# Moving the attention's weights by DMA into a one-pass tile before TensorE turns them

## The chip, the cores and the metric

The kernel runs on one core of a Trainium2 chip. The metric is device time in microseconds (us) of one execution. A core has a matrix engine (TensorE, PE in the profile, with its weight loads listed as PEld), a vector engine (VectorE, DVE), a scalar engine (ScalarE, ACT), a general engine (GpSimd, POOL) and a synchronisation engine (SyncE, SP). Each of them works off its own list of instructions in order and waits on semaphores that the others raise. DMA transfers are issued by an instruction on one of these engines (here SP, whose issues appear as SPq, and POOL) and then run by themselves on 16 DMA engines that all transfers share.

## The reference

One decoder layer in float32 on four sequences of 512 rows of width 512, with three sublayers, each behind a layer norm (without learned scale) and each added to the residual stream x:

```
q, k, v = x@Wq+bq, x@Wk+bk, x@Wv+bv       # 16 heads of width 128
y = softmax(q k^T / sqrt(128)) v          # here q, k are laid out so that the
x = x + y @ Wo + bo                       # softmax runs over feature pairs of a head
x = x + gamma * cross_attention(layernorm(x), ctx, ctx)      # 8 heads
x = x + (silu(h @ w1q') * (h @ w3q')) @ w2q',  h = layernorm(x)   # ternary weights
```

In the first sublayer the transposes put the 128 features of a head on both axes of the scores: for each sequence and head there is a 128 x 128 score matrix, summed over the 512 rows of the sequence. Its softmax is applied to the values, and the result goes through Wo. The change is in this sublayer alone, between its softmax and the product with Wo and the values.

## The kernel before, in words

**The attention.** The work is done per sequence b (0 to 3) and per group j (0 to 3) of four heads, so in 16 rounds. Since both axes of the scores are features, the kernel first forms the Gram matrix G of the normalised rows (`gram_upper`, matmuls `pg`, and `gram_rest`, which mirrors its lower blocks with TensorE transposes `gt`). A round then computes `u`, rows times Wo's part (`values_out`, PSUM names `pu`); `y`, G times Wk's part (`keys_of`, `py`); `m`, Wv's part times u (`values_of`, `pm`); and the scores (`scores`, line 503). `scores` takes Wq's part times y into one PSUM bank `sc` (L509, 16 matmuls of 128 x 128), finds the row maxima on DVE (L517), writes the exponentials to the tile `e` on ACT (L524, four, one for each head), and divides them by their row sums on DVE (L535, four, in place). `e` is 128 x 512: four heads side by side.

`turned` (L540) belongs to the next round: TensorE transposes the four 128 x 128 blocks of `e` into a PSUM bank `pe` (L126 in `transpose_blocks`, a matmul with `e`'s block as the loaded weights and the constant `ident` as the moving side), and ACT copies the bank to `eT`. `output` (L545) then multiplies `eT` with `m` (`po`) and adds to the accumulators `acc`. For j = 0, 1, 2 the four transposes stand between the `pu` and the `py` products of the following round; for j = 3 they stand inside the next sequence's Gram products, after `pg_1`, and for the last sequence after the loop.

**Number formats.** The larger products are made in TensorE's one-pass format (fp32r): every operand is split into a high part h, a low part l and a part d, so that a product of three such terms is as good as a float32 one (lines L336, L337, L348; `tri_of` makes the parts, ACT copies the first sum out of PSUM at L343 into a tile `t`, DVE totals the two at L358). The transposes, the scores, `po`, and some products of sequence 0 (L370) are in plain float32.

**Sequence 0** is special: it also prepares the weights. SP loads raw pieces of 256 KB (`load`, L196; `v_last`, `k_raw` and so on), DVE folds a correction into them (L255), ACT and DVE make the parts, and POOL issues the DMAs that keep them in DRAM for the later sequences (`keep`, L274) and small ones for the biases (L251). The output bias row is loaded once for each sequence into a tile `bo_bc` (`bias_rows`, L841; by SP for b = 0, by POOL for b > 0), and in sequence 0 it is added to the four accumulators by DVE in round j = 1 (`biased`, L857), between that round's totals of `u`.

**Buffers.** Tiles of one tag share slots in turn: a tile that takes a slot waits until the tile that was there before it has been read for the last time. The pool `a_y` (tag `y`, five slots of 128 x 512) holds a round's four `y`, the four blocks of G for b > 0, and `bo_bc`. The pool `a_t` has three slots (`t` copies and `u` totals), `e` has one slot of its own, and the eight PSUM banks go round in the same way.

**Order.** The order on each engine isn't that of the source. A planner places instructions by the modelled times of what they need (a few stretches are held in place by hand, with `issue_after` and `manual_schedule`). So a tile that asks for another slot can move instructions that the source doesn't touch, on every engine and in the DMA queues.

**The rest.** While sequences 1 to 3 go through the attention, the cross-attention of the sequence before (`xs`, `xp`, `xo`; its loads are POOL issues at L689) and the quantisation of the feed-forward weights are mixed in. At the end come the feed-forward products (L1084, L1119).

Of the kernel before, what the change touches and what calls it, by code (L numbers as in the profile page):

```python
# [11 lines left out]
F32 = mybir.dt.float32  # L12

F32R = mybir.dt.float32r
# [5 lines left out]
P = 128  # L20
B, T, D = 4, 512, 512
# [4 lines left out]
GW = HG * DH  # L26
# [13 lines left out]
def decoder_layer_kernel(  # L40
# [16 lines left out]
    nc = tc.nc  # L57

    const = ctx.enter_context(tc.tile_pool(name="const", bufs=1))
# [6 lines left out]
    def bank(name):  # L66
        return psum.tile([P, 512], F32, tag="bank", name=name)
# [8 lines left out]
        for n in ("w1", "w3", "w2")  # L76
    }
    scales = {n: const.tile([P, 3], F32, name=f"scales_{n}") for n in ("w1", "w3", "w2")}
    ident = const.tile([P, P], F32, name="ident")
    ones = const.tile([P, P], F32, name="ones")  # L80
    eps = const.tile([P, 1], F32, name="eps")
    gam = const.tile([P, 1], F32, name="gam")
# [39 lines left out]
    def transpose_blocks(dst, src, name, on_act):  # L122

        pt = bank(name)
        for k in range(4):
            nc.tensor.transpose(pt[:, ts(k, P)], src[:, ts(k, P)], ident)  # L126
        pv = pt.rearrange("p (k t) -> p k t", k=4)
        if on_act:
            nc.scalar.copy(dst, pv)  # L129
        else:  # L130
            nc.vector.tensor_copy(dst, pv)
# [18 lines left out]
    def apool(name, bufs):  # L150
        return apools.enter_context(tc.tile_pool(name=name, bufs=bufs))

    x3p, xnp, g3p, u3p = apool("a_x3", 12), apool("a_xn", 4), apool("a_g3", 1), apool("a_u3", 12)
    yp, tp = apool("a_y", 5), apool("a_t", 3)
# [60 lines left out]
    def exact(n, b, j):  # L215
        return b > 0 or j >= FIRST[n]
# [85 lines left out]
    def weights(n, b, j, wp):  # L302
        def wtile(name, dt=F32R):
            return wp.tile([P, GW], dt, tag="w", name=name)

        if n == "q":
            return [load(wtile(f"q_{b}_{j}_{k}", F32), kept_q[j][ts(k, P), :]) for k in range(KC)]
        tris = []
        make = b == 1 and not exact(n, 0, j)
        one = one_of(recent[0]) if make else None  # L310

        def part(p, k):
            t = wtile(f"{n}{p}_{b}_{j}_{k}")
            if p != "d" or not make:
                load(t.bitcast(F32), kept[n, j, p][ts(k, P), :])
            return t

        halves = [(part("h", k), part("l", k)) for k in range(KC)]
        for k in range(KC):
            tri = Tri(*halves[k], part("d", k))  # L320
            if make:
                nc.vector.scalar_tensor_tensor(
                    tri.d, tri.l.bitcast(F32), one, tri.h.bitcast(F32), ALU.mult, ALU.subtract
                )
                nc.gpsimd.dma_start(kept[n, j, "d"][ts(k, P), :], tri.d.bitcast(F32))
            tris.append(tri)
        return tris
# [57 lines left out]
    def normed(b, xs, by_chunk):  # L385

        mv = small.tile([P, NG, 2], F32, tag="mv", name=f"mv_a_{b}")

        def finish(part, std):
            rstd = inverse(std, f"a_{b}_{part[0]}")  # L390
            for g in part:
                normalize(xs[g], xs[g], mv[:, g, 0:1], rstd[:, g - part[0] : g - part[0] + 1])
                last = nc.vector.memset(xs[g][:, D - 1 : D], 1.0).ins
            return last

        parts = [(g,) for g in range(NG)] if by_chunk else [tuple(range(NG))]
        due = []
        for part in parts:
            for g in part:
                if b > 0:  # L400
                    settle(xs[g])
                moments(mv[:, g, :], xs[g], f"a_{b}_{g}")
            if b == 0:
                with tc.issue_after(mark["std"]):
                    nc.scalar.copy(accs[part[0]], xs[part[0]])
            due.append((part, std_of(mv[:, part[0] : part[-1] + 1, :], f"a_{b}_{part[0]}")))
            if len(due) > 1:
                finish(*due.pop(0))
        return finish(*due.pop())
# [93 lines left out]
    def scores(b, j, w, ys):  # L503

        scale = (S if exact("k", b, j) else 1.0) / math.sqrt(DH)
        sc = bank(f"sc_{b}_{j}")
        for g in range(NG):
            for k in range(KC):
                nc.tensor.matmul(  # L509
                    sc[:, ts(g, DH)],  # L510
                    lhsT=w[k][:, ts(g, DH)],
                    rhs=ys[k][:, ts(g, DH)],
                    start=(k == 0),
                    stop=(k == KC - 1),
                )
        nmax = small.tile([P, NG], F32, tag="nmax", name=f"nmax_{b}_{j}")
        mark["nmax"] = nc.vector.reduce_max(  # L517
            nmax, sc.rearrange("p (h k) -> p h k", h=NG), axis=AX.X
        ).ins
        nc.vector.tensor_scalar(nmax, nmax, -scale, None, ALU.mult)  # L520
        e = ep.tile([P, GW], F32, name="e")
        den = small.tile([P, NG], F32, tag="den", name=f"den_{b}_{j}")
        for g in range(NG):
            nc.scalar.activation(  # L524
                e[:, ts(g, DH)],
                sc[:, ts(g, DH)],
                AF.Exp,
                bias=nmax[:, g : g + 1],
                scale=scale,
                accum_out=den[:, g : g + 1],  # L530
            )
        rden = small.tile([P, NG], F32, tag="rden", name=f"rden_{b}_{j}")
        nc.vector.reciprocal(rden, den)
        for g in range(NG):
            nc.vector.tensor_scalar(  # L535
                e[:, ts(g, DH)], e[:, ts(g, DH)], rden[:, g : g + 1], None, ALU.mult
            )
        return e

    def turned(b, j, e):  # L540
        eT = ep.tile([P, NG, DH], F32, tag="eT", name=f"eT_{b}_{j}")
        transpose_blocks(eT, e, f"pe_{b}_{j}", True)
        return eT
# [136 lines left out]
    def cross(b, cx, cin, cpp, cpt):  # L680
# [71 lines left out]
        def transpose_rows(n, h, ps):  # L752
            if h == 0:
                pts[n] = cpt.tile([P, NC, T], F32, tag="pt", name=f"pt_{b}_{n}")
            for i in range(2):
                transpose_blocks(
                    pts[n][:, :, ts(2 * h + i, P)], ps[i], f"xp_{b}_{n}_{h}_{i}", i or h
                )

        def turn_values(c):  # L760
            vals[c] = cin.tile([P, NC, P], F32, tag="vals", bufs=1, name=f"vals_{b}_{c}")
            transpose_blocks(vals[c], rows[c], f"vt_{b}_{c}", True)
# [70 lines left out]
    accs = [accp.tile([P, D], F32, tag="acc", name=f"acc_0_{g}") for g in range(NG)]  # L833
    with tc.manual_schedule(engines={nc.vector.engine}):
        rows_done = normed(0, xs, True)
    make_identity(nc, ident)
    cpools = ctx.enter_context(ExitStack())

    def bias_rows(b):
# [25 lines left out]
    for j in range(HG):  # L865
# [58 lines left out]
        if j == HG - 1:  # L924
            normed(1, xs, False)
        e = scores(0, j, w, ys)
        keep_weights("q", j, w, first, gates["q"])
        if j == 0:
# [48 lines left out]
    for b in range(1, B):  # L977
# [18 lines left out]
        for j in range(HG):  # L996
            u3 = values_out(b, j, x3, weights("o", b, j, wp), tick)
            if j > 0:
                waiting[2] = turned(*waiting[:3])
            ys = keys_of(b, j, g3, weights("k", b, j, wp), tick)  # L1000
            if j > 0:
                output(*waiting)
            else:
                accs = accumulators(b, bo_bc)
            if j == HG - 2:
                xs = rows_of(b + 1)
            if j == HG - 1 and b + 1 < B:
                normed(b + 1, xs, False)
                x3 = parts_of(b + 1, xs)
            elif j == HG - 1:  # L1010
                for t in xs:
                    settle(t)
                ffn_0 = prepare_ffn(0, xs)
                for _ in range(NC):
                    next(ffn_0)
            ms = values_of(b, j, weights("v", b, j, wp), u3, tick)
            e = scores(b, j, weights("q", b, j, wp), ys)
            if j == 0:
                biased(accs, bo_bc)
            waiting = [b, j, e, ms, accs]  # L1020
# [48 lines left out]
    for b in range(B):  # L1069
# [39 lines left out]
        for c in range(NC):  # L1109
            if b == B - 1:  # L1110
                y = last_ys[c]
            else:
                y = fwk.tile([P, D], F32, tag="y", bufs=1, name=f"yo_{b}_{c}")
# [63 lines left out]
```

## Time and profile before

Three runs took 1152.76, 1149.95 and 1154.46 us; the median is 1152.76 us. The profiled execution spans 1150.0 us from its first to its last instruction.

| What | Value |
|---|---|
| Median of three runs | 1152.76 us |
| Runs, lowest to highest | 1149.95 to 1154.46 us |
| Span of the profiled execution | 1150.0 us, at a granted TensorE clock of 0.999 |
| PE busy | 1140.7 us, 99% of the span, 5310 matmuls |
| DVE busy | 818.7 us, 71% |
| ACT busy | 523.5 us, 46% |
| POOL busy | 295.9 us, 26% |
| Moved by DMA | 270.68 MB, mean 235 GB/s |

How to read the profile: a row of the timeline gives the start in us, the busy time in us, the engine, the line of the kernel, the operation, the output tile `<-` the inputs, and how many instructions are put together; a bracket at the end tells how long the engine stood idle before and what ended the wait. A row of a tile's view gives durations in ns as minimum/median/maximum, then the first and the last start. Matmuls overlap in the engine's pipeline: a matmul's own duration is longer than the step from one start to the next, and the step is what a row of many costs. A row of DMA issues gives the number of transfers, KB for each, and the median us from issue to landing. The chain is followed backwards from the last instruction, at each step to what released it.

### The profile page before, as it was taken

What the parts mean: (1) busy time and instruction counts of PE and PEld (TensorE: products, weight loads), DVE (VectorE), ACT (ScalarE), POOL (GpSimd) and SP (SyncE); (2) the same over time, 40 slices, a digit from 0 to 9 for tenths busy, and PEclk for the clock granted to TensorE, in tenths of its full rate; (3) what the DMA queues carried; (4) which work ended last, traced back from release to release, by engine and by line L of the source; (5) the groups of instructions that cost most, each with busy time, mean ns of one, the idle gap of its engine ahead of it and who ended that gap; (6) DMA issues with size and microseconds to landing.
All of it is one profiled execution on the core that took longest, in us unless ns stands there. A gap on an engine that the chain in (4) does not pass through costs nothing.

```text
span 1150.0 us, 16662 instructions
## 1 busy us (share of the span) xinstructions
PE 1140.7 (99%) x5310; PEld 858.6 (75%) x5310; DVE 818.7 (71%) x1818; ACT 523.5 (46%) x1071; POOL 295.9 (26%) x534
## 2 busy tenths in 40 slices
PE   9999999999999999999999999999999999999998
PEld 5486585787778767877776787777778877777886
DVE  6857766978788965969696769788857856536242
ACT  4534334354535442644354445445355768534020
POOL 3435433433133232213221422122113212000000
PEclk9999999999999999999999999999999999999999
DMA  9999996998889769988986798799791422122100
GB/s 332 306 344 337 345 314 225 324 319 280 281 281 308 261 201 325 312 272 276 321 291 215 256 334 271 254 330 325 268 304 40 122 79 65 48 73 72 64 1 37
DMA packets 146177, 270.68 MB, mean 235 GB/s; under 512 B 18276, under 2 KB 49300, under 8 KB 146090
## 3 DMA queue, kind: packets, MB, share of 16 engines
q1 hardware_dynamic: 112218, 164.93, 43.4%
q0 software_dynamic: 33872, 104.70, 26.8%
q8 instruction: 42, 0.69, 0.2%
q14 instruction: 45, 0.37, 0.1%
HBM read 206.62 MB, written 62.93 MB: 234 GB/s over the span
## 4 chain that ended last, share of the span: by engine, by line
PE 96%; DMA 2%; DVE 1%; issue 1%; ACT 0%; POOL 0%; SPq 0%; DVEq 0%; POOLq 0%; ACTq 0%
PE h L1084 13%; PE y L1119 7%; PE xo L770 5%; PE xp L126 5%; PE po L548 5%; PE pm L370 5%; PE sc L509 5%; PE pg L430 3%; PE xs L727 3%; PE xs L726 2%; PE pu_2h L336 1%; PE pu_1d L348 1%; PE py_3h L336 1%; PE py_3h L337 1%; PE pu_2h L337 1%; PE py_2h L337 1%
## 5 line engine op out<-in xcount | busy, mean ns | idle before, releaser
L1084 PE MATMUL h<-fxh,t 128*128 128x512 f32 (+1 forms) x352 | 139.6, 397 | 0.0
L1084 PE MATMUL h<-fxl,t 128*128 128x512 f32 (+1 forms) x352 | 137.4, 390 | 0.0
L737 ACT ACTIVATE p<-xs,xnmax 128x512 f32<-128x512 f32 x128 | 87.2, 689 | 84.8 <-PE xp L126 68.2
L731 DVE TENSOR_REDUCE xnmax<-xs 128x1 f32<-128x512 f32 x128 | 83.5, 684 | 19.3 <-PE xs L727 19.3
L1084 PEld LDWEIGHTS h<-fxh,t 128*128 128x128 f32 (+1 forms) x352 | 65.0, 185 | 15.4 <-issue 1.1
L1084 PEld LDWEIGHTS h<-fxl,t 128*128 128x128 f32 (+1 forms) x352 | 65.0, 185 | 14.7 <-issue 0.2
L1119 PE MATMUL y<-t,gh 128*128 128x512 f32 (+1 forms) x176 | 69.3, 394 | 0.0
L1119 PE MATMUL y<-t,gl 128*128 128x512 f32 (+1 forms) x176 | 68.8, 391 | 0.0
L129 ACT COPY pt<-xp 128x512 f32<-128x512 f32 x96 | 54.1, 595 | 31.0 <-PE xp L126 31.0
L126 PE MATMUL xp<-ident,p 128*128 128x128 f32 x512 | 66.5, 273 | 0.0
L126 PEld LDWEIGHTS xp<-ident,p 128*128 128x128 f32 x512 | 59.3, 140 | 9.4 <-issue 2.4
L770 PE MATMUL xo<-pt,vals 128*64 128x512 f32 x256 | 61.5, 599 | 0.0
L1097 DVE SCALAR_TENSOR_TENSOR gf<-h,scales_w,sl 128x512 f32<-128x512 f32 (+1 forms) x44 | 32.9, 747 | 39.8 <-PE h L1084 36.4
L749 DVE TENSOR_SCALAR p<-p,xrden 128x512 f32<-128x512 f32 x128 | 56.7, 486 | 2.9
L548 PE MATMUL po<-m,eT 128*128 128x512 f32 x128 | 57.6, 593 | 0.0
L1093 ACT ACTIVATE sl<-h,scales_w 128x512 f32<-128x512 f32 (+1 forms) x44 | 30.1, 688 | 58.7 <-PE h L1084 58.5
L689 POOL DMA_DIRECT2D xd<-x_a x64 | 33.8, 532 | 88.6 <-DVE qs L710 64.5
L370 PE MATMUL pm<-u,v_raw 128*128 128x512 f32 x128 | 55.6, 592 | 0.0
L727 PE MATMUL xs<-kl,qs 128*128 128x512 f32 x128 | 50.1, 391 | 0.5 <-DVE kl L714 0.5
L138 POOL CAST gh<-gf 128x512 fp32r<-128x512 f32 (+1 forms) x24 | 15.8, 660 | 134.9 <-DVE gf L1097 119.7
L726 PE MATMUL xs<-kh,qs 128*128 128x512 f32 x128 | 50.1, 392 | 0.0
L139 DVE TENSOR_TENSOR gl<-gf,gh 128x512 fp32r<-128x512 f32 (+1 forms) x44 | 30.4, 690 | 26.3 <-POOL gh L138 19.3
(313 smaller groups left out, 2897.6 us busy)
## 6 DMA issues: line engine op xcount, KB each, us to landing
oh<-kept_oh SPq DMA_DIRECT2D x48, 256.0 KB, 5.9
ol<-kept_ol SPq DMA_DIRECT2D x48, 256.0 KB, 6.2
kh<-kept_kh SPq DMA_DIRECT2D x48, 256.0 KB, 5.2
kl<-kept_kl SPq DMA_DIRECT2D x48, 256.0 KB, 5.9
vh<-kept_vh SPq DMA_DIRECT2D x48, 256.0 KB, 6.6
vl<-kept_vl SPq DMA_DIRECT2D x48, 256.0 KB, 6.9
q<-kept_q SPq DMA_DIRECT2D x48, 256.0 KB, 6.6
od<-kept_od SPq DMA_DIRECT2D x44, 256.0 KB, 6.8
```

Source lines behind the costliest of these rows:

```text
L126: nc.tensor.transpose(pt[:, ts(k, P)], src[:, ts(k, P)], ident)
L370: nc.tensor.matmul(p, lhsT=lhs(k)[:, ts(i, P)], rhs=rhs(k), start=(k == 0), stop=(k == 3))
L509: nc.tensor.matmul(sc[:, ts(g, DH)], lhsT=w[k][:, ts(g, DH)], rhs=ys[k][:, ts(g, DH)], start=(k == 0), stop=(k == KC - 1),)
L548: nc.tensor.matmul(po, lhsT=eT[:, g, :], rhs=ms[g], start=True, stop=True)
L726: nc.tensor.matmul(sc, lhsT=q[:, ts(m, P)], rhs=kh, start=True, stop=False)
L727: nc.tensor.matmul(sc, lhsT=q[:, ts(m, P)], rhs=kl, start=False, stop=True)
L731: nc.vector.reduce_max(nmax[:, i : i + 1], scs[i], axis=AX.X)
L737: nc.scalar.activation(p, scs[i], AF.Exp, bias=nmax[:, i : i + 1], scale=xscale, accum_out=den[:, i : i + 1],)
L749: nc.vector.tensor_scalar(ps[i], ps[i], rden[:, i : i + 1], None, ALU.mult)
L770: nc.tensor.matmul(po[half, :], lhsT=vals[c][:, l, half], rhs=pt[j][:, l, :], start=(l == 0), stop=(l == NC - 1),)
L1084: nc.tensor.matmul(ph[:r, :], lhsT=t[:, block(i, k)], rhs=fxT[j][:, k, :], start=(k == 0 and j == 0), stop=(k == KC - 1 and j == 1),)
L1119: nc.tensor.matmul(py, lhsT=g[i][j][:r, ts(c, P)], rhs=t2[:r, i, :], start=(i == 0 and j == 0), stop=(i == NHC - 1 and j == 1),)
```

## The change

The divided exponentials are copied by a DMA, issued on POOL, from `e` to a new tile `moved` (named `e_b_j`) of type fp32r in the `y` pool, and the transposes read `moved` in the one-pass format instead of `e` in float32. For that the identity matrix is needed as an fp32r tile: it is built in a float32 tile `eye` (also in the `y` pool) and copied by POOL to `ident_r`; `ident` becomes a float32 view of the same bytes, for all other transposes.

```diff
-    ident = const.tile([P, P], F32, name="ident")
+    ident_r = const.tile([P, P], F32R, name="ident")
+    ident = ident_r.bitcast(F32)
...
         pt = bank(name)
         for k in range(4):
-            nc.tensor.transpose(pt[:, ts(k, P)], src[:, ts(k, P)], ident)
+            if src.dtype == F32R:
+                nc.tensor.transpose(pt[:, ts(k, P)].bitcast(F32R), src[:, ts(k, P)], ident_r)
+            else:
+                nc.tensor.transpose(pt[:, ts(k, P)], src[:, ts(k, P)], ident)
...
                 e[:, ts(g, DH)], e[:, ts(g, DH)], rden[:, g : g + 1], None, ALU.mult
             )
-        return e
+        moved = yp.tile([P, GW], F32R, tag="y", name=f"e_{b}_{j}")
+        nc.gpsimd.dma_start(moved.bitcast(F32), e)
+        return moved
...
-    make_identity(nc, ident)
+    eye = yp.tile([P, D], F32, tag="y", name="eye")[:, :P]
+    make_identity(nc, eye)
+    nc.gpsimd.tensor_copy(ident_r, eye)
```

There are 16 such DMAs, each of 128 rows of 2 KB (256 KB), and 64 transposes that change their format. Only `e` is an fp32r source: the transposes of G, of the cross-attention and of the feed-forward inputs stay as they are. The change adds no slot to the `y` pool.

Line numbers in this document are those of the kernel before.

## The prediction

> **What bounds the kernel now.** I read the busy times first, then the clock slices and the chain, then the groups of the tiles `pe` and `y`, and last the timeline around the 16 turns.
>
> ```profile
> span 1150.0 us, 16662 instructions
> PE 1140.7 (99%) x5310; PEld 858.6 (75%) x5310; DVE 818.7 (71%) x1818; ACT 523.5 (46%) x1071; POOL 295.9 (26%) x534
> PEclk9999999999999999999999999999999999999999
> PE 96%; DMA 2%; DVE 1%; issue 1%; ACT 0%; POOL 0%; SPq 0%; DVEq 0%; POOLq 0%; ACTq 0%
> ```
>
> PE works through the whole span at full clock, and the chain is PE for 96%. The holes between its matmuls add up to some 4 us. So only two things move the time: PE work that becomes shorter, and any wait put ahead of a matmul. Everything else counts only where it makes PE wait.
>
> ```profile
> L126 PEld LDWEIGHTS pe<-ident,e x64: 138/140/143, 77.2 to 847.7; 128*128 128x128 f32 x64
> L126 PE MATMUL pe<-ident,e x64: 270/272/329, 77.4 to 847.7; 128*128 128x128 f32 x64
> 839.37 1.04 PE L126 MATMUL xp<-ident,p 128*128 128x128 f32 x8
> 81.54 1.98 PE L348 MATMUL py_1d<-k_d,gd 128*128 128x512 f32 x8
> ```
>
> The reader is to see the price of a turn (rows 2 and 3: eight take 1.04 us and the last is 272 ns long, so a step is (1.04−0.27)/7 = 110 ns) and of the one-pass format (row 4: (1.98−0.39)/7 = 227 ns for 512 columns).
>
> **What becomes shorter.** 64 turns change format. If 128 columns cost a quarter of 227 ns, a step is 57 ns: 64 × 52 = 3.3 us gained. No row has a one-pass product of 128 columns, so the ends lie far apart. One end is 3.3 us. In the middle is nothing: the step stays at 110 ns, limited by the weight load. The other end is a loss: a float32 product of that shape takes two halves of 112 ns in the scores, and at 224 ns the turns would cost 64 × 0.114 = 7.3 us more. I take the 3.3, by the nearest row of that format, and because the turn's weight load is shorter (140 ns) than the other loads of 128 columns (187 to 192).
>
> The Trainium skill, "TensorE: Matmul & The Clock Gate", section "LDWEIGHTS (loading the stationary operand)", speaks against that: a load costs its number of columns divided by 1.2, 107 ns for 128 columns, whatever the product behind it. By it the gain would be nothing and the sum below 3.3 us higher.
>
> **What is added.** Before, the turn reads `e` itself. Now a POOL DMA of 256 KB stands between, and `moved` takes the fifth slot of the `y` pool.
>
> *Waits for the DMA.* From the end of the division (L535) to the first turn there are 7.1 to 13.9 us in 14 of the 16 rounds. POOL's transfers of this size land in 2.3 to 3.8 us in quiet stretches, 4 to 7 in sequences 1 to 3, 6 to 8 in sequence 0. So 14 are hidden; closest are the first round of sequence 0 and of sequence 1 (about 1 us over), bounded at 0 to 1 us each, taken as 0. Two have no slack:
>
> ```profile
> 194.78 0.87 DVE L535 TENSOR_SCALAR e<-e,rden 128x128 f32<-128x128 f32 x4
> 196.10 0.60 PE L126 MATMUL pe<-ident,e 128*128 128x128 f32 x4
> 843.17 0.88 DVE L535 TENSOR_SCALAR e<-e,rden 128x128 f32<-128x128 f32 x4
> 843.60 0.63 PE L126 MATMUL pe<-ident,e 128*128 128x128 f32 x3
> 847.74 0.33 PE L126 MATMUL pe<-ident,e 128*128 128x128 f32 x1
> keys<-in_kv_dram POOLq DMA_DIRECT2D x1, 256.0 KB, 3.1
> bo_bc<-in_bo_dram POOLq DMA_DIRECT2D x1, 256.0 KB, 3.8
> xc<-x_a POOLq DMA_DIRECT2D x1, 256.0 KB, 7.1
> ```
>
> The last three are issues: two of 190 to 206 us, one of 838 to 856.
>
> - Sequence 0, j = 3: `e` is done at 195.65. An issue of 0.35 and a landing of 3.1 give 199.1, against 196.10: a stall of 3.0 us (2.2 with the quickest landing of 2.3, 3.8 with `bo_bc`'s 3.8). Behind the turns on PE stand the last two rows of the Gram matrix.
> - Sequence 3, j = 3: three turns before stood at 843.6, within the cross-attention, ahead of the last block's division. In the changed order all four stand together after `xo_3`, which PE reaches at about 847.4, so most of the latency is covered. `e` is done at 844.05; the issue comes behind `xc` on POOL's queue, and `xc` landed after 7.1 us at 848.2. A transfer behind it lands between 848.3 and 851.5: a stall of 0.9 to 4.1, I take 2.5. Nothing follows the turns on PE that could go ahead of them.
>
> *The bias row in sequence 0.* This is the largest part, and it isn't in the edited lines. With `e_0_0` in the fifth slot, `bo_bc_0` has to take that of `y_0_0_0`, and in the changed program its SP load goes from 45.00 us to behind the loads of `k_raw_2`, ahead of `v_last_2`. DVE's four additions of it (L857) move behind `u_1_1` and ahead of `u_1_2`.
>
> ```profile
> 45.00 0.65 SPq L841 DMA_DIRECT2D bo_bc<-in_bo_dram  x1
> 76.45 0.56 SPq L196 DMA_DIRECT2D v_last<-in_wv_dram  x1
> 61.88 0.68 DVE L857 TENSOR_TENSOR acc<-acc,bo_bc 128x512 f32<-128x512 f32 x1
> 62.55 1.89 DVE L857 TENSOR_TENSOR acc<-acc,bo_bc 128x512 f32<-128x512 f32 x3
> 72.03 1.29 DVE L358 SCALAR_TENSOR_TENSOR u<-pu_1t,pu_1d 128x512 f32<-128x512 f32 x2 [2.73 <-PE pu_1d L348]
> 77.43 0.60 PE L126 MATMUL pe<-ident,e 128*128 128x128 f32 x4
> 78.33 0.40 PE L336 MATMUL py_1h<-k_h,gh 128*128 128x512 f32 x1
> ```
>
> The load is issued at about 76.4 and lands at 81.1 (4.7 us, as `k_raw` and `v_last` beside it). The additions take 2.57 us and `u_1_2` 0.65: it is done at 84.4 instead of 72.7. Queued behind them on DVE are `u_1_3`, the gate and the four `v_raw` corrections. ACT waits as well: the copy `py_1t_1` needs the buffer of `t` that `u_1_2` reads, and the copy of `eT` stands behind it. PE does the four turns and two products of `py_1h_3`, and the third, at 78.33 before, needs the bank of `pu_1d_2` that `u_1_2` frees: a stall of 84.4 − 78.3 = 6.1 us. With a landing of 3.1 (POOL's quietest row of this size above) it is 4.5; with 11.2 (the `v_raw` loads at 58 to 66 us) 12.6. In the same stretch POOL's stores of the `k` parts (L274, five of them) and the DMA of `e_0_0` come some 10 us earlier than before, and the small bias DMAs (L251) follow them in the queue, which speaks for a landing in the upper half.
>
> *The clock behind that stall.* The only cold stretch of this trace is the first:
>
> ```profile
> 1.09 5.52 PE L232 MATMUL idle<-ones 128*128 128x128 f32 x32 [1.09 <-DVE sums_w L614]
> ```
>
> 32 products take 5.52 us where 32 × 0.11 = 3.5 would do, so getting to full clock costs 2.0 us. No hole of the trace exceeds 0.9 us, so whether 6 us of idleness lowers the clock isn't shown: 0 to 2.0, and I take 2.0 as the only row there is. The same page of the Trainium skill, section "Part 1: The HAM clock gate", has about 3.4 us of idleness as the point from which the clock is halved, until the engine has been busy as long; by that rule the drop comes here and perhaps not at the two shorter stalls, an estimate of 1.7 us for one.
>
> *Waits that get shorter.* PE waited 0.87 us for `vd` at 228 and 0.70 for `od` at 246, both for DMAs that do not depend on PE's progress. A PE that comes later absorbs up to 1.6; I take 0.8.
>
> **At nothing.** The copy of the identity stands on POOL at about 9 us and the first turn (`gt`) at 29.4. DVE's `less`, which reads the identity, moves to about 10.7, its first use is at 21.7. `bo_bc_1` on POOL now comes behind the DMA that loads `od` and waits for the turn of `e_0_3`: issued at about 200, needed by DVE at about 226. 16 issues of 0.54 us are 8.6 us on a POOL that is 26% busy; the later POOL DMAs (the stores, the cross-attention's loads) stand behind each `e` DMA's wait, but the planner has put it after the division's modelled end. 4 MB more at 270.68 MB is 1.5%, with DMA busy 0.71 on the mean. Small swaps on ACT, DVE and PE in sequences 1 to 3 move an Exp by some 0.6 us inside slacks of 7 and more. If one of these covers is gone, it costs up to a landing (4 to 7 us) in one round.
>
> **The sum**, against the profiled execution of 1150.0 us (2.8 under the median of the three runs):
>
> −3.3 (turns) + 6.1 (bias row) + 2.0 (clock) + 3.0 (end of sequence 0) + 2.5 (end of sequence 3) − 0.8 = +9.5 us, so 1159.5. On the median: 1152.8 + 9.5 = 1162.
>
> **Rivals.**
>
> - *The turn gets no cheaper.* For it: no row shows a step under 109 ns with a fresh load of 128 columns. Against it: no row has a product short enough to show one, and the shorter load. Then +12.8: 1165.6. With the loss of 7.3 instead, +20.1: 1173, which I hold for the less likely half of a half.
> - *The bias row comes in time, so not slower.* The place is SP's load of `bo_bc_0` in sequence 0. If SP's loads ahead of it go out earlier, since the `k` parts that free their slots are kept earlier, it lands earlier. From 75.0 on back there is no stall; landing by 79.4 makes it 4.4 without a clock drop, and the sum is then below the 0.5% (5.8 us) that a measurement of this kernel can tell from no change. With no stall at all: −3.3 + 3.0 + 2.5 − 0.8 = +1.4, 1154.2. Against it: the queue's order and `k_raw_2`'s wait for slots, which in the trace of before kept those issues to 74.84.
> - *Everything is hidden.* Then −3.3: 1149.5. It needs the two ends of sequences to find other work too, and the trace has `e` done 0.45 us ahead of the turn in the one and after its first turn in the other.
>
> **How the numbers follow.** Forecast 0.48, no cheaper turn 0.23 (all slower but a sliver), bias row in time 0.20 (nearly all within 0.5%), everything hidden 0.09 (on both sides of −0.5%, mostly within). So faster 0.03, same 0.24, slower 0.73. The range goes from below the bias-row case, 1153, to the second case with part of the stall's upper bound (1165.6 + 5.4), 1171; the likeliest case by itself has 1157 to 1168.
>
> **What would show it.** Right: the `pe` row's step falls to about 57 ns; a PE hole of some 6 us at 78 us in front of `py_1h`, released by DVE `u`, with `bo_bc`'s landing behind it; a clock digit below 9 after it; holes of 2 to 4 us before `pe` at 196 and 848, released by the DMA. Wrong: PE busy unchanged (turns no cheaper), `bo_bc` landed before 75 us, or stores and loads of later rounds slowed by the extra transfers, with holes before products that read kept parts.

## The result and the profile after

The changed kernel took 1171.58 us (median of four runs, 1170.05 to 1175.14) against 1152.44 us for the kernel before: a ratio of 1.0175, with a 95% interval of 1.0153 to 1.0196. The profiled execution spans 1168.2 us against 1150.0, so it shows 18.2 of the 19.1 us (it is the fastest of the four runs, 1170.05 us). The forecast was 1162 with a range to 1171; slower was right, the size was half of what came.

The page's first lines, the clock slices and the chain of the changed kernel:

```profile
span 1168.2 us, 16723 instructions
PE 1144.1 (98%) x5310; PEld 858.5 (73%) x5310; DVE 818.8 (70%) x1818; ACT 523.0 (45%) x1071; POOL 304.9 (26%) x551
PEclk9988999999999999999999999999999999999999
PE 92%; DMA 5%; DVE 1%; issue 1%; ACT 1%; SPq 0%; POOL 0%; ACTq 0%; POOLq 0%; DVEq 0%
```

PE has the same 5310 matmuls, and DMA has grown from 2% to 5% of the chain. The two 8s are slices three and four, 58 to 117 us. The view of the waits, PE's longest (us in all, times, longest):

```profile
PE py_1h L340 <- DVE u L362: 9.7, 1, 9.7
PE pe L128 <- DMA e<-e: 5.2, 3, 2.8
PE py_0d L352 <- DMA kd<-kept_kd: 1.0, 2, 0.6
PE pu_1d L352 <- DMA od<-kept_od: 1.0, 1, 1.0
```

The first two are new: one wait of 9.7 us for DVE's total of `u`, and three for the DMA of `e`, at 77.6, 209 and 863 us (0.32, 2.05 and 2.83 us). Line numbers from here on are those of each kernel's own trace; the changed kernel has the `u` total at L362, the additions of the bias row at L865, its load at L849 and the turns at L128.

The timeline of the changed kernel around the largest wait, and the turns at the ends of sequences 0 and 3:

```profile
74.11 4.83 SPq L200 DMA_DIRECT2D q_raw<-in_wq_dram  x4
78.61 0.39 PE L341 MATMUL py_1h<-k_l,gl 128*128 128x512 f32 x1
79.04 1.40 SPq L200 DMA_DIRECT2D k_raw<-in_wk_dram  x2
80.49 0.71 SPq L849 DMA_DIRECT2D bo_bc<-in_bo_dram  x1
85.56 2.50 DVE L865 TENSOR_TENSOR acc<-acc,bo_bc 128x512 f32<-128x512 f32 x4 [17.56 <-DMA bo_bc<-in_bo_dram]
87.97 1.28 DVE L362 SCALAR_TENSOR_TENSOR u<-pu_1t,pu_1d 128x512 f32<-128x512 f32 x2
88.71 0.79 PE L340 MATMUL py_1h<-k_h,gh 128*128 128x512 f32 x1 [9.71 <-DVE u L362]
94.45 1.75 PE L352 MATMUL py_1d<-k_d,gd 128*128 128x512 f32 x7
211.05 0.53 PE L128 MATMUL pe<-ident,e 128*128 128x128 f32 x4 [2.05 <-DMA e<-e]
866.25 0.50 PE L128 MATMUL pe<-ident,e 128*128 128x128 f32 x4 [2.83 <-DMA e<-e]
```

The chain that was forecast is there link by link: the bias row's load stands behind `k_raw` on SP, DVE's additions wait 17.56 us for it, `u_1_2` follows them, and PE's third product of `py_1h_3` waits for its bank. But the load went out at 80.49 us, where the forecast had 76.4.

Since PE runs the same matmuls in nearly the same order, the lag of the changed kernel behind the one before can be read at the same matmul in both traces. Its growth gives the account, in us of the profiled executions:

| Where | Forecast | Measured |
|---|---|---|
| 64 turns in the new format | −3.3 | −1.2 |
| Wait for the bias row in sequence 0 | +6.1 | +9.9 |
| Half clock behind it | +2.0 | +2.5 |
| End of sequence 0 | +3.0 | +2.2 |
| End of sequence 3 | +2.5 | +2.6 |
| Everything else | −0.8 | +2.3 |
| Sum | +9.5 | +18.3 |

The lag is 0.53 us ahead of the third product of `py_1h_3` and 10.38 at it (9.9); twelve products later, and at `py_1d` (94.45 us, 81.54 before), it is 12.91 (2.5). It goes from 12.74 to 14.95 at the turn that ends sequence 0 and from 16.17 to 18.76 at the one that ends sequence 3. The turns' term is the time from the start of the second matmul ahead of four turns to the end of the second step behind them: 1362 ns before and 1289 after where the neighbours are `py` products, 1516 and 1440 in the Gram products, 1123 and 1046 behind `xp`. That is 73 to 77 ns for four, some 19 ns for each turn. The last term is what is left.

Where the load lost its time is in the DMA queues of 59 to 76 us (packets, MB, share of 16 engines; q1 is SP's, q0 POOL's). Before:

```profile
q1 hardware_dynamic: 5183, 2.71, 55.1%
q0 software_dynamic: 1109, 3.50, 51.1%
```

The changed kernel, same window:

```profile
q0 software_dynamic: 1549, 5.08, 74.3%
q1 hardware_dynamic: 3108, 1.63, 31.4%
```

In both the DMA engines were busy almost without a break. POOL moved 1.58 MB more in these 17 us: the stores of the `k` parts that stood at 77.9 to 80.1 us before stand at 67 to 71, and `e_0_0` behind them. SP got 1.08 MB less, and its issues stretched. The difference arises behind 67 us: from 59 to 67 us POOL moved 2.18 MB before and 2.15 after, SP 0.96 and 0.95. In the timeline of the changed kernel, and below it of the one before, three loads of `v_raw`:

```profile
59.50 11.22 SPq L200 DMA_DIRECT2D v_raw<-in_wv_dram  x3
```

```profile
59.07 7.09 SPq L196 DMA_DIRECT2D v_raw<-in_wv_dram  x3
```

They ended 4.6 us later, and everything behind them in SP's queue, the bias row too, went out 4 us late. But these three loads are not what marks the cause: the second of them was already held up from 62.15 to 67.51 us, ahead of the moved stores. In a second profile of the changed kernel they took about as long as before, the four `q_raw` loads behind them took 9.05 us instead of 5.05, and the bias row went out just as late:

```profile
59.36 7.42 SPq L200 DMA_DIRECT2D v_raw<-in_wv_dram  x3
69.49 9.05 SPq L200 DMA_DIRECT2D q_raw<-in_wq_dram  x4
80.28 0.79 SPq L849 DMA_DIRECT2D bo_bc<-in_bo_dram  x1
```

What goes with the stores is the delay as a whole. Take the load that follows the last two `k_raw` on SP: `v_last` before, the bias row in the changed order. In the five profiles of this document in which five stores of `k` parts stand at 77 us or later it went out at 76.4 to 77.3 us, in the four in which three of these stores and the DMA of `e_0_0` stand at 68 to 74 us at 78.6 to 79.6, and in the four of the changed order, in which all five and the DMA stand ahead, at 80.3 to 80.9. So the earlier POOL transfers and the later load go together in 13 profiles. That it is the bytes, and not some slot that SP's loads wait for, is argued: the profile doesn't tell what held each issue, and no run changes the stores alone.

### The profile page after: what moved, and what is told of

It is laid out like the page before. It is cut to its first block, busy times and chain, and to the rows that moved or that the text cites. A ratio compares the mean times of both kernels' runs of the same rounds, so it can differ in the third digit from the quotient of the medians.

```text
span 1168.2 us, 16723 instructions
## 1 busy us (share of the span) xinstructions
PE 1144.1 (98%) x5310; PEld 858.5 (73%) x5310; DVE 818.8 (70%) x1818; ACT 523.0 (45%) x1071; POOL 304.9 (26%) x551
## 4 chain that ended last, share of the span: by engine, by line
PE 92%; DMA 5%; DVE 1%; issue 1%; ACT 1%; SPq 0%; POOL 0%; ACTq 0%; POOLq 0%; DVEq 0%
PE h L1092 13%; PE y L1127 7%; PE xo L776 5%; PE xp L130 5%; PE po L554 5%; PE pm L374 5%; PE sc L513 5%; PE pg L434 3%; PE xs L732 2%; PE xs L733 2%; DMA kd<-kept_kd 1%; PE pu_2h L340 1%; PE py_3h L340 1%; PE py_2h L340 1%; PE py_3h L341 1%; PE pu_2h L341 1%
```

## The experiments

Diffs are against the changed kernel unless another is named. All ratios are to the kernel before, measured on the same chip in the same series of runs.

### The bias row ahead of the scores

```diff
+        if j == 0:
+            bo_bc = bias_rows(0)
         e = scores(0, j, w, ys)
         keep_weights("q", j, w, first, gates["q"])
         if j == 0:
-            bo_bc = bias_rows(0)
```

> The changed kernel with the bias row of sequence 0 asked for ahead of the scores of round 0, so that bo_bc_0 has the fifth y slot again and e_0_0 takes that of y_0_0_0: the bias row's load and its four additions stand where they stood before the change; the DMA and the one-pass turns stay. If the slot and the cold clock behind it are the largest part (my theory): the hole of 9.7 us at 79 us and the 2.6 us of half clock behind it are gone, the waits ahead of pe at the ends of sequences 0 and 3 (2.0 and 2.8 us) stay: 1171.6 - 12.3 = 1159.3 us, between 1158 and 1161. If the hole is owed to the 16 added DMAs and their traffic instead (rival), it stays in another place: about 1171.

Measured: 1169.33 us, ratio 1.0156 (1.0140 to 1.0173). The load was back at 45.14 us and the additions ended at 64.6, and yet only 1 to 2 us were won against the two series of the changed kernel (1171.58 and 1170.63). My theory, that the slot was the cause and its undoing would do, fell in this form: the hole had moved to the place ahead of the turn. POOL's issues and PE in this kernel's timeline:

```profile
69.17 0.52 POOL L255 DMA_DIRECT2D v_raw<-in_bqkv_dram  x1 [0.19 <-issue]
77.40 0.53 POOL L255 DMA_DIRECT2D q_raw<-in_bqkv_dram  x1 [7.72 <-PE py_1d L352]
79.51 0.54 POOL L543 DMA_DIRECT2D e<-e  x1
83.49 0.72 PE L128 MATMUL pe<-ident,e 128*128 128x128 f32 x4 [5.68 <-DMA e<-e]
```

With the bias row's additions back in their place, the planner also put POOL's issues back to where they were, and the DMA of `e_0_0` came to stand behind the small bias load of `q_raw`, ahead of which POOL waited 7.72 us. `e` had been done at 67.0 us; its DMA was issued at 79.51, landed after 3.84 us, and PE waited 5.68 us and then ran slowly (the products behind the turns lie 0.43 us apart instead of 0.23, at a granted clock of 0.57 from 83 to 89 us). In the changed kernel that issue had stood at 71.47. So each of the planner's two orders has one of the two late: the bias row, or `e`.

### The bias loads behind the DMA of e

Against the kernel of the experiment above:

```diff
-            nc.gpsimd.dma_start(heads(chunks[KC - 1][P - 1 :, :]), of_heads(bias, j))
+            moved = mark.get(("moved", j - (2 if n == "k" else 1))) if n != "v" else None
+            with tc.issue_after(moved) if moved is not None else nullcontext():
+                nc.gpsimd.dma_start(heads(chunks[KC - 1][P - 1 :, :]), of_heads(bias, j))
...
-        nc.gpsimd.dma_start(moved.bitcast(F32), e)
+        done = nc.gpsimd.dma_start(moved.bitcast(F32), e).ins
+        if b == 0:
+            mark["moved", j] = done
```

> The kernel of the bias-row-first experiment (1169.3 us) with POOL's small bias loads for q and k in sequence 0 ordered behind the DMA of e of the round before, which had stood behind them and behind four stores there and was issued at 79.5 us. Theory: it is this place in POOL's queue that keeps the hole of 5.7 us ahead of the first turn, and the half clock of some 2.3 us behind it goes with it: 1169.3 - 8.0 = 1161.3 us, between 1160 and 1163, with e landing by 77 us. Rival: the transfer itself is slow in that stretch, where the DMA engines are busy throughout, and lands past 79 us wherever it stands in the queue: 1165 or more.

Measured: 1160.26 us, ratio 1.0072 (1.0056 to 1.0089), within the expected 1160 to 1163. The timeline:

```profile
70.89 0.54 POOL L545 DMA_DIRECT2D e<-e  x1 [0.26 <-issue]
78.08 0.46 PE L128 MATMUL pe<-ident,e 128*128 128x128 f32 x4
```

`e_0_0` landed at 76.7 us, PE didn't wait, and no clock was lost there. The place in the queue was the cause, not the transfer's speed: it took 5.84 us in the busy stretch and was hidden all the same. Both orders together are worth some 10 us of the 19 (1170.63 against 1160.26 in the same series).

### No DMA at the two ends

Against the kernel of the experiment above:

```diff
+        if j == HG - 1 and b in (0, B - 1):
+            return e
         moved = yp.tile([P, GW], F32R, tag="y", name=f"e_{b}_{j}")
```

> The kernel with both orders mended, and in the two rounds that end sequence 0 and sequence 3 no DMA: there the float32 turn reads e directly, as before the change. Theory: the two waits of 2.0 and 2.6 us and what half clock there is behind them go as well, the other 14 DMAs are hidden, and the turns' gain (19 ns each by the step over four turns in the traces, so 56 x 19 ns = 1.1 us) is all that is left: 1151 to 1154 us against 1152.2 before. Rival: the added DMAs cost time in the other rounds too (slower loads of kept parts): 1155 or more.

Measured: 1155.38 us, ratio 1.0036 (1.0023 to 1.0048). The two waits were worth 4.9 us by the medians. In the changed kernel's trace they read 2.2 and 2.6; in the profile of the kernel above, which still has them, the second is followed by a stretch at a lower clock as well (0.61, the third number from the end; ahead of it the row has the window, its length, and the busy time and count of PE, PEld, DVE, ACT and POOL, behind it the DMA share and GB/s):

```profile
854.00:858.00 4.00, 4.00 (x10) 2.19 (x9) 2.21 (x4) 2.61 (x4) 0.79 (x2) 0.61 0.48 122
```

What is left is still 3.6 us above the kernel before, on the rival's side: with every DMA landed ahead of its turn and no wait for `e` in the profile, the change doesn't even reach the old time.

### Is it the traffic?

The kernel with both orders mended and all 16 DMAs, but the turns read `e`:

```diff
         if b == 0:
             mark["moved", j] = done
-        return moved
+        return e
```

> The kernel with both orders mended (bias row first, bias loads behind the DMA of e), in which all 16 DMAs of e to a tile of the y pool are still made, but nobody reads that tile: the turns read e itself in float32. It takes away every wait for the DMA and leaves its traffic, its places in POOL's queue and its slots. Theory: the version with 14 DMAs stood 3.6 us above the one without any (1155.4 against 1151.8 us, and 1151.9 against 1148.3 by the profiled spans), in waits for loads of kept parts and not for e; so traffic and queue cost that much: 1155 to 1157 us, the undone one-pass turns (1.1 us) included. Rival: what costs is that the turns depend on the DMA: 1152.

Measured: 1152.82 us, ratio 1.0005 (0.9996 to 1.0014). My theory that it was the traffic and the queue fell. 4 MB more, 16 issues on POOL and 16 transfers that nobody waits for cost nothing that these runs tell from zero.

The kernel without DMAs at the two ends, with the 14 turns reading `moved` in float32:

```diff
-        moved = yp.tile([P, GW], F32R, tag="y", name=f"e_{b}_{j}")
+        moved = yp.tile([P, GW], F32, tag="y", name=f"e_{b}_{j}")
-        done = nc.gpsimd.dma_start(moved.bitcast(F32), e).ins
+        done = nc.gpsimd.dma_start(moved, e).ins
```

> The kernel with both orders mended and no DMA at the two ends, but with moved in float32 and float32 turns that read it: the 14 turns still depend on the DMA and hold its slot, only their format is undone. It stands between the version with 14 one-pass turns (1155.4 us, 3.6 above before) and the one whose 16 DMAs nobody reads (1152.8, 1.3 above). Theory: holding a slot of the y pool until the turn, and with it later loads and products, costs about 2.5 us in small waits: then 1156.5 us, the 1.1 us of the turns' gain included. Rival: the 1155.4 was a matter of that chip's runs and the cost is the traffic's alone: 1153.

Measured: 1155.67 us, ratio 1.0037 (1.0025 to 1.0049). So what costs 3 to 4 us is that the turns use the moved tile, not that it is filled, and the format makes no difference that can be told here. The waits of this kernel:

```profile
PE py_0d L354 <- DMA kd<-kept_kd: 2.1, 3, 0.8
PE xt_f L975 <- ACT sl L1108: 1.7, 1, 1.7
PE pu_1d L354 <- DMA od<-kept_od: 1.4, 1, 1.4
PE pe L130 <- DMA e<-e: 0.4, 1, 0.4
```

One turn in 14 waited 0.4 us for its DMA in this execution; the other three rows are waits for loads of kept parts and one ahead of `xt_f`, each longer than before (1.0 for `kd`, 0.7 for `od`, 0.6 for `xt_f`). Whether they come from the slot, which is now held from the DMA to the turn, or from a turn that is now and then late wasn't separated; the kernel whose DMAs nobody reads has some of them as well (1.9 for `kd` in its profile, which is the slowest of its eleven runs, 1155.53 us), so that one profiled execution doesn't settle it.

### The clock behind the wait

```diff
         pt = bank(name)
+        if name == "pe_0_0":
+            for _ in range(40):
+                nc.tensor.matmul(pt[:, :P], lhsT=ones, rhs=ones, start=True, stop=True)
         for k in range(4):
```

> The changed kernel with 40 float32 products of ones on the first turn's bank, ahead of the first four turns (8.8 us of PE work in a hole of 9.7 us; their results are overwritten by the turns). Theory: the hole is ended by the bias row on DVE and not by PE, and the 12 products behind it ran at half clock since PE had stood still: with the fill the time gets 2.0 to 2.7 us shorter, about 1169.1 us, though PE does 8.8 us more. Rival: the products behind the hole are slow for another reason (their operands or the bank): no difference, 1171.6, or with the fill on the path up to 1180.

Measured: 1166.90 us, ratio 1.0135 (1.0120 to 1.0151); the span is 1165.6 us against the changed kernel's 1168.2. PE's timeline, and the windows of 77 to 89 and 89 to 94 us, with the granted clock again third from the end:

```profile
77.51 9.09 PE L128 MATMUL pe<-ones 128*128 128x128 f32 x80
88.46 0.50 PE L343 MATMUL py_1h<-k_h,gh 128*128 128x512 f32 x1 [1.03 <-DVE u L365]
```

```profile
77.00:89.00 12.00, 10.97 (x91) 10.36 (x91) 3.69 (x6) 0.50 (x2) 1.02 (x2) 1.00 0.55 164
89.00:94.00 5.00, 5.00 (x22) 3.94 (x21) 4.25 (x10) 2.35 (x6) 0.00 (x0) 1.00 0.07 22
```

The same second window in the changed kernel:

```profile
89.00:94.00 5.00, 5.00 (x13) 3.85 (x13) 4.49 (x10) 0.82 (x2) 0.00 (x0) 0.50 0.06 19
```

22 matmuls instead of 13 in the same 5 us, at a clock of 1.00 instead of 0.50: idleness had halved the clock, and 9.09 us of idle work on PE made the kernel faster. The medians say 3.7 us (against 1170.63 for the changed kernel in a second series), the spans 2.6, the lag in the trace 2.5.

### The price of a turn

The DMA and its slots, but float32 turns:

```diff
-        moved = yp.tile([P, GW], F32R, tag="y", name=f"e_{b}_{j}")
-        nc.gpsimd.dma_start(moved.bitcast(F32), e)
+        moved = yp.tile([P, GW], F32, tag="y", name=f"e_{b}_{j}")
+        nc.gpsimd.dma_start(moved, e)
```

> The changed kernel with the moved tile in float32 and the turns in float32: slots, DMA and order as in the changed kernel, only the format of the 64 turns is undone. The turn's step in the changed trace is 83 ns against 109, so 64 x 26 = 1.7 us: 1173.2 us if the turns' price is on the path all the time. Rival: the turn's gain is swallowed by the waits that follow (PE only waits longer), then 1171.6, no difference.

The one-pass turns, but no DMA:

```diff
-        e = ep.tile([P, GW], F32, name="e")
+        er = ep.tile([P, GW], F32R, name="e")
+        e = er.bitcast(F32)
...
             nc.scalar.activation(
-                e[:, ts(g, DH)],
+                er[:, ts(g, DH)],
...
             nc.vector.tensor_scalar(
-                e[:, ts(g, DH)], e[:, ts(g, DH)], rden[:, g : g + 1], None, ALU.mult
+                er[:, ts(g, DH)], e[:, ts(g, DH)], rden[:, g : g + 1], None, ALU.mult
             )
-        moved = yp.tile([P, GW], F32R, tag="y", name=f"e_{b}_{j}")
-        nc.gpsimd.dma_start(moved.bitcast(F32), e)
-        return moved
+        return er
```

> The changed kernel without the moved tile and its DMA: the exponentials and the division write a tile e of the one-pass type, so they are rounded to it (the output has that error), and the one-pass turns read it directly. Slots and order are those of before. Theory: nothing is left but the turns' gain, 64 x 26 ns = 1.7 us: 1152.4 - 1.7 = 1150.7 us, and the pe step is 83 ns. Rival: the 83 ns of the changed trace come from the tile's place or from what stands behind, and the turn on its own shows 57 ns: 1149.1; or no gain, 1152.4.

Measured: 1170.06 us, ratio 1.0162 (1.0147 to 1.0177), for the first, the time of the changed kernel within the runs' scatter; 1151.84 us, ratio 0.9999 (0.9988 to 1.0011), for the second. In times both are inconclusive, since 64 turns hold too little. In the traces they agree: the step over four turns is 1362 ns with float32 and 1289 with one-pass turns, in either kernel. The one-pass turns and the product behind them start 60, 62, 89 and 83 ns apart, the float32 ones 108, 108, 109 and 28; that is 59 of the 73 ns, and the rest lies in the steps beside. So the price was measured where it is eight times as much, on the 512 turns of the cross-attention:

```diff
-                p = cpp.tile([P, T], F32, tag="p", name=f"p_{b}_{n}_{h}_{i}")
+                p = cpp.tile([P, T], F32R, tag="p", name=f"p_{b}_{n}_{h}_{i}")
...
-                nc.vector.tensor_scalar(ps[i], ps[i], rden[:, i : i + 1], None, ALU.mult)
+                nc.vector.tensor_scalar(
+                    ps[i], ps[i].bitcast(F32), rden[:, i : i + 1], None, ALU.mult
+                )
...
-        moved = yp.tile([P, GW], F32R, tag="y", name=f"e_{b}_{j}")
-        nc.gpsimd.dma_start(moved.bitcast(F32), e)
-        return moved
+        return e
```

> Neither the moved tile nor its DMA: e is turned in float32 as before. Instead the cross-attention's 512 turns of p are made in the one-pass format, p being written in the one-pass type by the exponential and the division (so it is rounded to it, and the output has that error). It measures the turn's price where it is eight times as much as in the change. By the four-turn steps of the changed trace (1289 against 1362 ns, 18 ns for each): 512 x 18 = 9.3 us less, 1143 us. By the one-pass rate for long products (57 ns against 109), 26 us less, 1126 us. By a weight load that sets the step: no difference, 1152.

Measured: 1142.09 us, ratio 0.9917 (0.9903 to 0.9930): 9.7 us for 512 turns, 19 ns each, as the four-turn step has it. The two forms of the turn, first before, then in this kernel, in the view of the tile (ns, minimum/median/maximum):

```profile
L126 PEld LDWEIGHTS xp<-ident,p x512: 137/140/224, 259.4 to 1022.3; 128*128 128x128 f32 x171
L126 PE MATMUL xp<-ident,p x512: 270/272/328, 259.6 to 1022.4; 128*128 128x128 f32 x171
```

```profile
L128 PEld LDWEIGHTS xp<-ident,p x512: 137/139/227, 260.9 to 1014.8; 128*128 128x128 f32 x171
L128 PE MATMUL xp<-ident,p x512: 222/247/307, 261.1 to 1014.8; 128*128 128x128 f32 x171
```

The matmul has become 25 ns shorter and the weight load hasn't changed. Within the runs of eight turns the starts are 80 ns apart in the mean, where they were 109; part of that is given back at the step to the product behind the run.

### A version that beats both

The two last edits together: `e` and `p` are written in the one-pass type by the instructions that make them, and nothing is moved.

> No moved tile and no DMA; both the 64 turns of e and the cross-attention's 512 of p are made in the one-pass format, e and p being written in the one-pass type by the exponentials and the divisions (both are rounded to it). If the turn's price holds: 1142.1 us for p alone and 64 x 18 ns = 1.2 us less: 1141 us, ratio 0.990, faster than both kernels. Rival: the gain for p is eaten up with that for e, where waits for loads come next: 1142 to 1143.

Measured: 1140.91 us, ratio 0.9908 (0.9895 to 0.9922), 10.6 us below the kernel before. It pays with a rounding of the softmax weights of both attentions to the one-pass type, as the expectation says, where the change's DMA copies the float32 bytes as they are. No run here measures that error; who can't accept it can't have this gain.

### The changed kernel once more

> The changed kernel as it is, on the same chip as the other runs, for a direct comparison: 1171.6 us as measured at first; 1168 to 1173 if chips differ by as much as the runs of the kernel before do.

Measured: 1170.63 us (1169.17 to 1174.33), ratio 1.0167 (1.0150 to 1.0184), as at first. In its profile the two waits in sequence 0 split as 1.52 us for `e` and 7.83 for `u` instead of 0.32 and 9.71, and the clock fell once more, behind the wait at the end of sequence 3 (3.0 us there).

## Why the prediction was right or wrong

Three steps of the prediction failed, all in the same direction: the bias row's issue "at about 76.4" (80.5 measured), the 52 ns gained for a turn (19 measured), and the 14 DMAs called hidden and costed at nothing (3 to 4 us measured without the other costs).

**What bounds the kernel** was right: the only gains and losses are in PE's steps and in the waits ahead of it, DVE and ACT have the same busy times as before, and POOL has 9.0 us more, for 16 issues that were put at 8.6.

**The turns** were priced wrongly, at 52 ns gained each; it is 19. The step that failed is the choice between the ends "by the nearest row of that format", 227 ns for 512 columns. A quarter of a long product is not the price of a short one: the product got shorter, but the steps are 60 to 89 ns, and 9.7 us for 512 turns confirm the mean. The rival of no gain leaned on a misreading too, that no row shows a step under 109 ns with a fresh load: before the change the product behind the fourth turn at 77 us, with a load of its own, starts 28 ns after it. The rule that the prediction weighed against this row (the Trainium skill, "TensorE: Matmul & The Clock Gate", section "LDWEIGHTS (loading the stationary operand)": 107 ns for a load of 128 columns) would have had no gain. Its sum was nearer than mine, but the 512 turns, each with a load of 128 columns of its own, start 80 ns apart in the mean, which is below it, and the measurement decides.

**The bias row** was the largest term as forecast, and by the mechanism forecast, link by link. What failed is the sentence "The load is issued at about 76.4": I took the load's new place in SP's queue from the changed order, and its time from the trace of before. The same part says that POOL's stores come some 10 us earlier, and used that for the landing alone; the issues in front of it are late wherever the stores are early, in eight profiles against five. The landing was 5.05 us (4.7 taken), the additions 2.5 (2.57 taken), the issue 4.1 us later: with PE itself 0.5 us later, that is the difference between 6.1 and 9.9. The rival that the row comes in time let the earlier stores speed SP's loads up; they went with later loads, and it fell.

**POOL's place of the `e` DMAs** was costed at nothing. In the changed kernel that held, if barely: the DMA of `e_0_0` stood 4.7 us behind stores (done at 66.8, issued at 71.47), and PE waited 0.32 us for it. In the kernel with the bias row first it stood 12.5 us, and PE waited 5.68. The forecast didn't see that the two go together.

**The clock** was right in kind and nearly in size, 2.5 to 2.6 us for 2.0 taken. The row at the start of the kernel was a fair stand-in for the size; here PE worked 5.3 us at half clock. At the two shorter stalls the sum had no such cost. In the execution of the table there was none, but in five of the six profiles with a wait at the end of sequence 3, the second one of the changed kernel among them, the clock halved behind it for another 1.2 to 1.7 us, and in one of six at the end of sequence 0.

**The ends of sequences 0 and 3** were right: 2.2 and 2.6 us for 3.0 and 2.5. The first landed after 2.31 us, the lower bound, with the DMA engines at 0.23 of their time from 208 to 211 us; the second after 5.94 us behind `xc`. Taking them out gave 4.9 us.

**Everything else** was costed at −0.8 and came to +2.3. The wait for `vd` at 228 us did go (−1.1 in the lag), but `od` at 246 (0.9), `kd` at 452 (0.7) and some later places (1.1 at 655 to 668) took more. "At nothing" held for the traffic, as the kernel whose DMAs nobody reads shows (1152.8). It didn't hold for the 14 dependences called hidden, of which the two closest were "bounded at 0 to 1 us each, taken as 0"; they cost 3 to 4 us in the two kernels that have them and nothing else; where they cost it, and why, stays open.

**The sum**: three terms missed in the same direction, 2.1 for the turns, 3.8 for the bias row and 3.1 for the rest, and 0.5 for the clock; the ends gave 0.7 back. The range reached the case of dear turns with part of the late landing, 1171; what came had two thirds of the first, and a late issue in place of the second, so that the range's end comes near the measured time by luck.

## What to carry to other kernels

A tile that asks for one more turn of a shared pool moves loads and additions that have nothing to do with it: read the changed order on every queue, and price a moved DMA from its issue, with what is now in front of it on all queues, not from the time at which its neighbour was issued before. An extra copy in front of an engine that is 99% busy has to be hidden in every round, and one round that isn't cost more here (2.2 and 2.6 us) than all 64 turns gave (1.2); where a rounding is acceptable, the format was to be had without it, by letting the instruction that writes the tile write it in that type. And a price that no row shows is best measured where there is most of it: 512 turns told in one run what 64 could not.

## What the runs showed of the hardware

- TensorE's clock halved after an idle stretch of 9.7 us, and 13 matmuls took the time of 22. It also halved after as little as 2.03 us: in the kernel with the bias row first, the turn at the end of sequence 0 was followed by a window at 0.50, while the changed kernel's window after the same wait (2.05 us) was at 1.00. The windows of 208 to 211 us of the one and 211 to 214 us of the other:

```profile
208.00:211.00 3.00, 3.00 (x9) 2.46 (x9) 3.00 (x6) 0.58 (x1) 0.77 (x2) 0.50 0.23 87
```

```profile
211.00:214.00 3.00, 2.95 (x20) 2.74 (x21) 3.00 (x5) 0.96 (x2) 0.48 (x2) 1.00 0.23 87
```

- So whether a wait of 2 to 3 us costs its own length or more differs between executions. Six profiles here have the waits at the ends of sequences 0 and 3, of 2.03 to 3.10 us. The clock halved behind one of the six at the first place and behind five of the six at the second, and the lag then grew by another 1.2 to 1.7 us; behind the rest, one of 2.83 us among them, it stayed at 1.00. The Trainium skill, "TensorE: Matmul & The Clock Gate", section "Part 1: The HAM clock gate", has some 3.4 us of idleness as the point from which the clock drops; here it dropped after 2.03 in one execution and not after 2.83 in another.
- A DMA from SBUF to SBUF of 256 KB issued by POOL landed in the changed kernel after 2.3 us in a quiet stretch (the end of sequence 0) and after 6.4 to 7.5 us in the busy ones of sequence 0, much as stores of that size did there (6.4 to 6.6 us in the median).
- Where the DMA engines are busy almost throughout, 1.58 MB more from POOL in 17 us went with 1.08 MB less of SP's loads, some of which had been issued earlier (1.18 MB more and 0.73 MB less in the second profile).
- The one-pass turn of 128 x 128 costs 19 ns less than the float32 one (512 turns: 9.7 us), with the same weight load (139 against 140 ns).
